# Copying transposed attention probabilities out of PSUM on two engines by turns

## The chip, the cores and the metric

The kernel runs on one core of a Trainium2 chip. That core has five engines that run beside each other, each with its own queue of instructions: TensorE (matrix products and transposes; in the profile PE, with PEld for its weight loads), VectorE (DVE), ScalarE (ACT), GpSimd (POOL) and SyncE (SP), which here issues DMAs. Matrix products land in PSUM, from where VectorE or ScalarE copies them to SBUF. The metric is the device time of one execution in microseconds (us); the figure for a kernel is the median of several executions.

## What is computed

Two layers of gated cross attention and feed forward on `x` of shape (2, 2048, 512) with a context of 128 rows per batch. The part that matters here is the first cross attention, with 16 heads of width 32 and biases on queries, keys and values:

```
q = (LN(x) Wq + bq) in 16 heads          # 2 x 2048 rows
k, v = ctx Wkv + bkv in 16 heads         # 2 x 128 rows
att = softmax(q k^T / sqrt(32)) over the 128 context rows
x = x + tanh(g_xattn[0]) * ((att v) Wo + bo)
```

After it `x` goes to a layer that picks 256 rows of each batch by a router score, runs self attention and a feed forward on them, and adds the result back; then comes a second cross attention (16 heads of width 64, no bias), and a feed forward of 2048 hidden units with rounded weights and values.

## The kernel before

The rows of x are worked in 8 blocks of 512 rows (4 tiles of 128). `cross_attention` (L215 on) is one function for both attentions; the flag `bias` is true for the first and false for the second. It loops over U, which counts heads over all blocks: 16 heads per block, 128 in all. One turn of the loop does these steps, for heads at different points of their way:

- `scores` (L268): TensorE multiplies queries by keys into `sc`. In the first attention four heads share a 128-row slice of the queries, so that the scores of four heads are made at once.
- `probabilities` (L285) calls `softmax_rows` (L116): VectorE takes the negated row maxima `nmx` (L119); ScalarE does four exponentials with running sums `den` (L122); VectorE inverts them into `rden` (L130); GpSimd multiplies `A` by `rden` (L131).
- Once per block `front` (L234) normalizes and transposes the rows of the next block; once per group of four heads `queries` (L246) makes `qT`, which ScalarE scales out of PSUM (L261).
- `transposed` (L291), two heads behind: TensorE transposes the four 128 x 128 pieces of `A` into one PSUM tile `tp` (L294), and `tp` is copied to `AT` in SBUF (L295).
- `values` (L297), after each fourth head: TensorE multiplies the four `AT` by the values into `po` (L302), and ScalarE copies `po` to `OT` (L310).
- `back` (L312), at the end of a block, in pieces: the output product `pp` (L320) and the gated residual sum (L329).
- `beside`: other work that is slipped in between. In the first attention this is the router (`router`, L795): statistics (L804, L805), scores (L808), the rows stored and the next rows loaded (L785, L832, L839), then the ranking of rows by comparisons on VectorE (`marks` L860, `tie` L904), and for the first batch's picked rows the self attention (L445 on).

The PSUM tiles `tp` and `po` come from one pool `ps_o` with two buffers (tag "o"; L741), and the router's `pb`, `old`, `new`, `pi` use the same two. `AT` has six SBUF buffers. A buffer is written again only when its last reader is done, so a transpose waits for the copy of the tile two before it.

The kernel is written against a tile framework that sets all waits between engines, and its planner fixes the order of every engine's queue ahead of the run. That order differs from the order of the program text: the trace shows, for example, the maxima of two later heads in VectorE's queue before the reciprocal of an earlier one. Each queue then runs in the order given.

Of the kernel before, what the change touches and what calls it, by code (L numbers as in the profile page):

```python
# [43 lines left out]
def flamingo_kernel(ctx: ExitStack, tc: tile.TileContext, a: dict, out: bass.AP):  # L44
    nc = tc.nc
# [169 lines left out]
    def cross_attention(  # L215
# [8 lines left out]
        L, nE, bias = W.L, W.nE, W.bias  # L224
# [9 lines left out]
        def front(n):  # L234

            tiles, xn, residual = rows_of(n)
            mv, rstd = ln_stats(tiles, L + "ln")
            for i, t in enumerate(tiles):
                normalize(xn[i], t, mv, rstd, i)
            xnT = act.tile([P, DC, BLK], F32, name="xnT", tag="xnT", bufs=xnT_bufs)  # L240
            transpose_block(
                ps_mm, "mm", xn, lambda d, pt: nc.scalar.copy(xnT[:, d, :], pt)
            )
            return residual, xnT

        def queries(xnT, grp):  # L246

            qT = [act.tile([P, BLK], F32, name="qT", tag="qT", bufs=3) for _ in range(cpg)]
            for c in range(cpg):
                e = grp * cpg + c  # L250
                pq = ps_mm.tile([P, BLK], F32, name="pq", tag="mm")
                for d in range(DC):
                    nc.tensor.matmul(  # L253
                        pq,
                        W.wq[:, d, ts(e, P)],
                        xnT[:, d, :],
                        start=(d == 0),
                        stop=(d == DC - 1),
                    )
                if bias:  # L260
                    nc.scalar.activation(  # L261
                        qT[c], pq, AF.Identity, scale=scale, bias=W.bq[:, e : e + 1]
                    )
                else:
                    nc.scalar.activation(qT[c], pq, AF.Copy, scale=scale)
            return qT

        def scores(b, qT, e):  # L268

            sc = [ps_sc.tile([P, TB, M], F32, name="sc", tag="sc") for _ in range(hpc)]
            for t in range(TB):
                for h in range(hpc):
                    r = slice(h * dh, (h + 1) * dh)
                    nc.tensor.matmul(  # L276
                        sc[h][:, t, :],
                        qT[e % cpg][r, ts(t, P)],
                        W.kT[r, b, e, :],
                        start=True,  # L280
                        stop=True,
                    )
            return sc

        def probabilities(sc):  # L285

            A = act.tile([P, TB, M], F32, name="A", tag="A", bufs=4)
            softmax_rows(sc, TB, M, act, row, A)
            return A

        def transposed(A, AT):  # L291
            tp = ps_o.tile([P, TB, P], F32, name="tp", tag="o")
            for t in range(TB):
                nc.tensor.transpose(tp[:, t, :], A[:, t, :], ident)  # L294
            nc.vector.tensor_copy(AT, tp.rearrange("p t n -> p (t n)"))  # L295

        def values(b, AT, OT, grp):  # L297
            for c in range(cpg):
                po = ps_o.tile([P, BLK], F32, name="po", tag="o")
                for h in range(hpc):  # L300
                    hd = grp * 4 + c * hpc + h
                    nc.tensor.matmul(  # L302
                        po[h * dh : (h + 1) * dh, :],
                        W.v[:, b, ts(hd, dh)],
                        AT[c * hpc + h],
                        start=True,
                        stop=True,
                    )
                OT.append(hold.tile([P, BLK], F32, name="OT", tag="OT", bufs=nE + cpg))
                nc.scalar.copy(OT[-1], po)  # L310

        def back(n, residual, OT):  # L312

            tiles = residual()
            for t in tiles:
                tc.keep_in_program_order(nc.gpsimd.tensor_tensor(t, t, W.bo, ALU.add))
            for i, t in enumerate(tiles):
                pp = ps_mm.tile([P, D], F32, name="pp", tag="mm")
                for e in range(nE):
                    nc.tensor.matmul(  # L320
                        pp,
                        OT[e][:, ts(i, P)],
                        W.wo[:, e, :],
                        start=(e == 0),
                        stop=(e == nE - 1),
                    )
                    if e == nE // 2 - 1:
                        yield
                nc.vector.scalar_tensor_tensor(t, pp, W.g, t, ALU.mult, ALU.add)  # L329
                if i == TB - 1:  # L330
                    after_block(n, tiles)
                yield
# [9 lines left out]
        As, AT, OT, out_of = {}, {}, {}, iter(())  # L342
        for U in range(N * H + 12):
            n, u = divmod(U, H)
            if n < N:
                grp, t = divmod(u, 4)
                if t == 0:
                    qT = next_qT
                if u % hpc == 0:
                    sc = scores(n // NBLK, qT, u // hpc)  # L350
                As[U] = probabilities(sc[u % hpc])
                if u == ahead and n + 1 < N:
                    residual[n + 1], xnT[n + 1] = front(n + 1)
                if t == 1 and grp < 3:
                    next_qT = queries(xnT[n], grp + 1)
                elif t == 1 and n + 1 < N:
                    next_qT = queries(xnT[n + 1], 0)
            V = U - 2
            if 0 <= V < N * H:
                AT[V] = act.tile([P, BLK], F32, name="AT", tag="AT", bufs=6)  # L360
                transposed(As.pop(V), AT[V])
            V = U - 4
            if 0 <= V < N * H and V % 4 == 3:
                n, grp = divmod(V // 4, 4)
                if grp == 0:
                    OT[n] = []
                values(n // NBLK, [AT.pop(i) for i in range(V - 3, V + 1)], OT[n], grp)
                if grp == 3:
                    out_of = back(n, residual.pop(n), OT.pop(n))
                    if n == N - 1:  # L370
                        after_units()
            next(out_of, None)
            beside(u)
# [369 lines left out]
    with ExitStack() as st:  # L743
# [43 lines left out]
        def beside(u):  # L787

            for _ in range(2):
                while pending and next(pending[0], pending) is pending:  # L790
                    pending.pop(0)
            for q in selecting:
                next(q, None)
# [211 lines left out]
        def stage1_rows(n):  # L1005
            tiles = [x[t] for t in range(n * TB, (n + 1) * TB)]
            xn = [act.tile([P, D], F32, name="xn", tag="xn", bufs=TB) for _ in tiles]
            return tiles, xn, lambda: tiles

        cross_attention(  # L1010
            W0, act, act, ps_mm, ps_sc, ps_o, row, 1, 10, stage1_rows,
            lambda n, tiles: pending.append(router(n, tiles)), beside,
# [319 lines left out]
    def quantize_hidden(g):  # L1332
# [27 lines left out]
        for c in range(HC):  # L1360
# [10 lines left out]
            if c % 2:  # L1371
                yield

    cross_attention(
        W1, act, hold, ps_mm, psum_pool(units, "L1_sc", 3), psum_pool(units, "L1_o", 2), row,
        1, 10, stage3_rows, stage3_done, beside4, second_half_starts,
# [51 lines left out]
    for g in range(LAST + 1):  # L1428
# [5 lines left out]
        for i in range(TB):  # L1434
            t, r, p = ahead.pop(0)
# [78 lines left out]
```

## Time and profile before

| | us |
|---|---|
| median of 3 executions | 1804.85 (1802.63 to 1807.84) |
| profiled execution, its own time | 1800.29 |
| its span, first to last instruction | 1798.6 |
| busy in the span: PE / DVE / ACT / POOL | 1648.9 / 1282.8 / 1070.5 / 537.6 |
| granted TensorE clock, mean | 0.967 of full |
| first copy `AT` starts; last copy of the first attention starts | 42.1; 542.4 |
| last copy `AT` of the second attention starts | 1574.7 |

Busy time is the sum of the durations of an engine's instructions; the ends of matrix products are modelled. Idle time of an engine counts only where something on the way to the end waits for it. The profile also gives, for each group of instructions of one line, the mean duration and what ended the idle time before them ("releaser"), and a chain of waits: starting at the last instruction, at each step back to what released it, or to the instruction before it on its engine. In the timelines "x4" stands for four like instructions in a row, taken together.

### The profile page before, as it was taken

To read this page: it belongs to the slowest core of one execution; us is meant where nothing else is said; L and a number is where in the kernel's file an instruction comes from. 1 tells how busy PE (TensorE), PEld (TensorE's weight loads), DVE (VectorE), ACT (ScalarE), POOL (GpSimd) and SP (SyncE) were. 2 spreads that over 40 slices of the span, in tenths; PEclk is the share of its full clock that TensorE was granted. 3 is DMA by queue.
4 is the path that set the end of the run, shared out by engine and by line. 5 is a ranking of instruction groups with operands and counts; after the bars stand their busy time and mean duration, and the time that the engine had idled before them with its cause. 6 is when DMAs were issued, how large, how long until landed. Compare 5 with 4: busy or idle time off the path is not lost.

```text
span 1798.6 us, 25225 instructions
## 1 busy us (share of the span) xinstructions
PE 1648.9 (92%) x8076; PEld 866.4 (48%) x8122; DVE 1282.8 (71%) x2608; ACT 1070.5 (60%) x3106; POOL 537.6 (30%) x671
## 2 busy tenths in 40 slices
PE   6998888989999988999999999999999999888969
PEld 3544444445455655755454544445444454434423
DVE  4676888966767534345358888798798879786967
ACT  2755456445453323435367878788788788744566
POOL 2534443432431012023224242342424324231200
PEclk9999999989889989999999999999999999998989
DMA  6011111121015880730011334234243133256375
GB/s 214 7 65 48 42 60 65 36 88 53 19 42 162 292 268 1 247 86 24 18 54 70 115 100 144 88 126 144 79 150 100 77 115 109 88 187 238 133 237 188
DMA packets 119828, 196.99 MB, mean 110 GB/s; under 512 B 12900, under 2 KB 50532, under 8 KB 115984
## 3 DMA queue, kind: packets, MB, share of 16 engines
q1 hardware_dynamic: 117872, 192.23, 31.2%
q0 software_dynamic: 960, 2.10, 0.6%
q8 instruction: 64, 1.05, 0.2%
q10 hardware_dynamic: 864, 1.05, 0.2%
q14 instruction: 68, 0.56, 0.1%
HBM read 120.89 MB, written 74.45 MB: 109 GB/s over the span
## 4 chain that ended last, share of the span: by engine, by line
PE 56%; DVE 23%; DMA 8%; ACT 6%; POOL 3%; issue 2%; SPq 0%; ACTq 0%; DVEq 0%; POOLq 0%
PE pp L320 14%; PE pq L253 12%; PE po L302 4%; PE sc L276 4%; PE tp L294 4%; PE ph L1157 3%; DVE h L1173 3%; DVE AT L295 2%; ACT A L122 2%; DVE nmx L119 2%; PE po L1386 2%; DVE marks L860 2%; PE pu L646 2%; PE acc L631 2%; PE pw L646 2%
## 5 line engine op out<-in xcount | busy, mean ns | idle before, releaser
L122 ACT ACTIVATE A<-sc,nmx 128x128 f32<-128x128 f32 x1024 | 363.2, 382 | 143.1 <-DVE nmx L119 129.5
L131 POOL TENSOR_TENSOR A<-A,rden 128x512 f32<-128x512 f32 x256 | 277.2, 1085 | 512.4 <-DVE rden L130 402.4
L320 PE MATMUL pp<-L_wo,OT 128*128 128x512 f32 x768 | 367.5, 610 | 16.6 <-DVE x L329 11.2
L253 PE MATMUL pq<-xnT,L_wq 128*128 128x512 f32 x768 | 346.6, 599 | 11.4 <-DVE x L329 11.4
L122 ACT ACTIVATION_READ_ACCUMULATOR A<-sc,nmx 128x1 f32 x1024 | 227.1, 222 | 0.0
L253 PEld LDWEIGHTS pq<-xnT,L_wq 128*128 128x128 f32 x768 | 143.2, 192 | 171.7 <-issue 151.0
L119 DVE TENSOR_REDUCE nmx<-sc 128x4 f32<-128x512 f32 x256 | 168.9, 679 | 69.8 <-PE sc L276 69.8
L320 PEld LDWEIGHTS pp<-L_wo,OT 128*128 128x128 f32 x768 | 136.7, 193 | 162.6 <-issue 132.8
L295 DVE COPY AT<-tp 128x512 f32<-128x512 f32 x256 | 172.9, 680 | 57.8 <-PE tp L294 56.9
L1173 DVE SCALAR_TENSOR_TENSOR h<-u,cw,h 128x512 f32<-128x512 f32 x256 | 204.5, 834 | 5.9 <-ACT h L1169 5.5
L294 PE MATMUL tp<-ident,A 128*128 128x128 f32 x1024 | 164.5, 284 | 25.4 <-POOL A L131 13.9
L294 PEld LDWEIGHTS tp<-ident,A 128*128 128x128 f32 x1024 | 118.2, 143 | 96.4 <-issue 46.0
L276 PEld LDWEIGHTS sc<-L_kT,qT 32*128 32x128 f32 (+1 forms) x2048 | 110.8, 190 | 75.8 <-issue 56.6
L276 PE MATMUL sc<-L_kT,qT 32*128 32x128 f32 (+1 forms) x2048 | 138.2, 292 | 6.5 <-ACT A L122 4.6
L1386 PE MATMUL po<-w2q,hq 128*128 128x512 bf16 x501 | 120.8, 393 | 18.4 <-DVE hq L1368 8.3
L1169 ACT ACTIVATE h<-u,cb,cw 128x512 f32<-128x512 f32 x128 | 99.1, 808 | 64.7 <-DVE u L1167 56.6
L1157 PE MATMUL ph<-xiT,w1q 128*128 128x512 bf16 x477 | 122.3, 379 | 3.8 <-DVE u L1167 1.8
L302 PE MATMUL po<-AT,L_v 128*32 128x512 f32 (+1 forms) x512 | 117.6, 646 | 7.7 <-DVE AT L295 6.2
L1167 DVE TENSOR_TENSOR u<-ph,inv_b 128x512 f32<-128x512 f32 x128 | 85.1, 684 | 31.5 <-PE ph L1157 27.5
L1166 POOL COPY u<-carry 128x2 f32<-128x2 f32 x128 | 49.7, 390 | 166.9 <-DVE h L1173 140.9
L310 ACT COPY OT<-po 128x512 f32<-128x512 f32 x96 | 56.0, 590 | 64.9 <-PE po L302 64.6
L1168 POOL COPY carry<-u 128x2 f32<-128x2 f32 x128 | 48.7, 385 | 149.7 <-DVE u L1167 147.9
(237 smaller groups left out, 2310.2 us busy)
## 6 DMA issues: line engine op xcount, KB each, us to landing
h_d<-h SPq DMA_DIRECT2D x28, 1024.0 KB, 4.4
x_d<-x SPq DMA_DIRECT2D x64, 256.0 KB, 3.2
hf<-h_d SPq DMA_DIRECT2D x64, 256.0 KB, 3.4
x<-x_d SPq DMA_DIRECT2D x61, 256.0 KB, 4.4
x<-h_d SPq DMA_DIRECT2D x48, 256.0 KB, 5.2
x_d<-xo SPq DMA_DIRECT2D x32, 256.0 KB, 2.0
xf<-x_d SPq DMA_DIRECT2D x32, 256.0 KB, 3.5
hq_d<-hi SPq DMA_DIRECT2D x64, 128.0 KB, 1.8
```

The lines of the kernel that those rows point to most:

```text
L119: nc.vector.tensor_reduce(nmx, sc, AX.X, ALU.max, negate=True)
L122: nc.scalar.activation(out_tile[:, h, :], sc[:, h, :], AF.Exp, bias=nmx[:, h : h + 1], accum_out=den[:, h : h + 1],)
L131: nc.gpsimd.tensor_tensor(out_tile, out_tile, rden.unsqueeze(2).to_broadcast([P, n, width]), ALU.mult,)
L253: nc.tensor.matmul(pq, W.wq[:, d, ts(e, P)], xnT[:, d, :], start=(d == 0), stop=(d == DC - 1),)
L276: nc.tensor.matmul(sc[h][:, t, :], qT[e % cpg][r, ts(t, P)], W.kT[r, b, e, :], start=True, stop=True,)
L294: nc.tensor.transpose(tp[:, t, :], A[:, t, :], ident)
L295: nc.vector.tensor_copy(AT, tp.rearrange("p t n -> p (t n)"))
L302: nc.tensor.matmul(po[h * dh : (h + 1) * dh, :], W.v[:, b, ts(hd, dh)], AT[c * hpc + h], start=True, stop=True,)
L320: nc.tensor.matmul(pp, OT[e][:, ts(i, P)], W.wo[:, e, :], start=(e == 0), stop=(e == nE - 1),)
L1157: nc.tensor.matmul(ph, w1q[:, d, ts(c, P)], xiT[g][:, d, :], start=(d == 0), stop=(d == DC - 1),)
L1173: nc.vector.scalar_tensor_tensor(z, u[:, ds(k, BLK)], cw[:, c, k : k + 1], z, ALU.mult, ALU.add)
L1386: nc.tensor.matmul(po, rows(c), w2q[:, c, :], start=(c == 0), stop=(c == HC - 1))
```

## The change

`transposed` gets the copying instruction as an argument. In the first attention (`bias` true) heads with an odd number V are copied by ScalarE's copy; heads with an even number, and all heads of the second attention, are copied by VectorE as they were.

```diff
-        def transposed(A, AT):
+        def transposed(A, AT, copy):
             tp = ps_o.tile([P, TB, P], F32, name="tp", tag="o")
             for t in range(TB):
                 nc.tensor.transpose(tp[:, t, :], A[:, t, :], ident)
-            nc.vector.tensor_copy(AT, tp.rearrange("p t n -> p (t n)"))
+            copy(AT, tp.rearrange("p t n -> p (t n)"))
...
             V = U - 2
             if 0 <= V < N * H:
                 AT[V] = act.tile([P, BLK], F32, name="AT", tag="AT", bufs=6)
-                transposed(As.pop(V), AT[V])
+
+                copy = nc.scalar.copy if bias and V % 2 else nc.vector.tensor_copy
+                transposed(As.pop(V), AT[V], copy)
```

No other line differs. The copies have the same shape, 128 x 512 in float32, and the same source and target tiles.

## The prediction

> **What bounds the kernel now.** I read the busy table of the page first: over the whole span TensorE is busy 92%, VectorE 71%, ScalarE 60%. The change touches only the first cross attention, so these means say little, and I cut the span by time. The 128 heads of that stage put their copies `AT` between 42 and 542 us. Busy time in three stretches, in the order PE, PEld, DVE, ACT, POOL, then granted clock, DMA share and GB/s:
>
> ```profile
> 45.00:180.00 135.00, 122.37 (x809) 65.53 (x808) 94.22 (x217) 87.29 (x394) 59.25 (x56) 0.99 0.11 40
> 180.00:360.00 180.00, 157.33 (x1026) 82.23 (x1022) 154.27 (x335) 94.38 (x415) 76.61 (x66) 0.98 0.15 51
> 360.00:540.00 180.00, 162.73 (x910) 90.17 (x911) 118.65 (x279) 91.21 (x383) 65.84 (x62) 0.90 0.15 51
> ```
>
> TensorE works 442.4 of these 495 us, so 52.6 us are the most that any relief of other engines could bring here. From 180 to 360 us VectorE is as full as TensorE (154.3 beside 157.3 of 180) and ScalarE is half empty (94.4). The two engines that the change trades between are thus unequal, and most so there.
>
> Then the groups of the page, for prices (operation, shapes, count | busy us, mean ns | idle before):
>
> ```profile
> L122 ACT ACTIVATE A<-sc,nmx 128x128 f32<-128x128 f32 x1024 | 363.2, 382 | 143.1 <-DVE nmx L119 129.5
> ...
> L295 DVE COPY AT<-tp 128x512 f32<-128x512 f32 x256 | 172.9, 680 | 57.8 <-PE tp L294 56.9
> ...
> L310 ACT COPY OT<-po 128x512 f32<-128x512 f32 x96 | 56.0, 590 | 64.9 <-PE po L302 64.6
> ```
>
> L295 is the copy that moves; L310 is the same shape, PSUM to SBUF, already done by ScalarE.
>
> Third, the chain of waits from 40 to 530 us, listed whole: PE holds 239 of its 491 us, DVE 140, ACT 45. L295 is on it with 35 copies, 21.4 us. I numbered the copies in order of time (the k-th is head k): 23 are odd heads, 12 even. The pieces look like this (start, us, what):
>
> ```profile
> 226.70 0.69 DVE ln_st L804
> 227.40 0.59 DVE AT L295
> 227.98 0.09 DVE ln_mv L805
> 228.07 0.58 DVE ws L808 x2
> ...
> 237.11 0.06 DVE rden L130
> 237.18 0.59 DVE AT L295
> 237.76 0.14 issue
> 237.90 0.63 PE tp L294 x4
> ...
> 265.84 0.60 DVE AT L295
> 266.44 0.60 DVE L_ln_st L99
> ```
>
> The first and the last (heads 57, 67) stand between VectorE's own instructions: nobody waits for that `AT`, it only holds up what is queued behind it. The middle one (head 59) is a real dependency: its buffer of the two-buffer PSUM pool is what the next transposes need. Of the 23 odd copies 16 are of the first kind, 7 of the second (heads 11, 27, 43, 47, 59, 75, 97).
>
> Fourth, who keeps TensorE waiting from 45 to 540 us (total us, times, longest):
>
> ```profile
> PE pp L320 <- DVE x L329: 10.8, 3, 4.3
> PE tp L294 <- POOL A L131: 10.4, 8, 3.2
> PE tp L294 <- DVE AT L295: 9.0, 8, 2.0
> ```
>
> So VectorE's queue, and not the length of one copy, is what TensorE feels: a residual add that comes late, a normalization whose `rden` came late, a copy that came late.
>
> **The change, part by part.** *Removed from VectorE*: 64 copies (odd V, first attention only). One lasts 0.68 us by its row, but the next instruction begins 0.60 us after it in the chain, so its place in the queue costs 0.60: 64 x 0.60 = 38.4 us, a tenth of the 367.15 us that the table gives VectorE.
>
> *Added to ScalarE*: 64 copies at 0.59 us (L310). What one occupies is read where it stands among exponentials:
>
> ```profile
> 242.72 0.21 ACT L122 ACTIVATION_READ_ACCUMULATOR A<-sc,nmx 128x1 f32 x1
> 242.81 0.60 ACT L873 COPY sb<-pb 128x512 f32<-128x512 f32 x1
> 243.28 0.40 ACT L122 ACTIVATE A<-sc,nmx 128x128 f32<-128x128 f32 x1
> ```
>
> The next one starts 0.47 us later: 64 x 0.47 = 30 us, so ScalarE goes from 272.88 to about 303 of 495 us, 61%. It does not become the bound. That L873 copy lies between two exponentials with nothing loaded in between, so the alternation itself is free.
>
> A rule speaks against this trade. The Trainium skill, "ScalarE: Activation LUTs", section "Rules for kernel authors", gives plain arithmetic to VectorE because VectorE is faster per element. By the rule each moved copy would be slower than the one it replaces. The rows say the opposite for this source: 590 ns on ScalarE beside 680 ns on VectorE, 0.09 us less. I take the rows. By the rule the 7 dependent copies would lose something each; by the rows they gain 7 x 0.09 = 0.6 us before queues are counted.
>
> *The 16 queue pieces on the chain.* Each leaves VectorE's queue and nothing has to follow at once: 16 x 0.60 = 9.6 us. What is late next? In the stretch about head 57 the chain runs on from L808 through POOL's `ln_rstd`, ScalarE's `xo`, a store and a load of x, to L99; VectorE waits 1.3 us for that load, TensorE 0.98 us for POOL and 1.46 us for `AT` there. A gain of 0.6 us fits under these waits. In the stretch from 252 to 272 us VectorE is full, TensorE idles 2.88 and 1.22 us; again 0.6 to 1.2 us fit. So little is cut off, and I take 8 of the 9.6 us.
>
> *The 7 dependent pieces.* The timeline has the transposes of head 59 end at 233.93 us, but the copy starts at 237.09: 3.2 us in VectorE's queue, behind maxima and L99. ScalarE ends the exponentials of head 61 at 234.75 (head 61 is what stands before this copy in program order), so there it would run from about 234.8 to 235.3. The next transposes then wait for POOL's `A` of head 61 (done at 237.53) instead and start 0.37 us earlier than their 237.90. Heads 27, 43 and 75 are the same place in other blocks: 4 x 0.37 = 1.5 us. Head 97 waits 4.5 us for VectorE and holds TensorE's L81 for 2.3 us of its own waits; head 47 holds L866 for 1.2 us, and head 11's copy begins 0.8 us after its transposes end. Best case: 1.5 + 2.3 + 1.2 + 0.8 = 5.8 us gained. Worst case: the planner puts these copies behind the exponentials of heads 62 and 63 (end 238.1), so that they end 0.75 us later than now: 7 x 0.75 = 5 us lost. I take -2, nearer to the first end, since the copy stands before those exponentials in program order.
>
> *The wait that is added to ScalarE.* A copy waits for PE's transposes, and behind it on ScalarE stand the exponentials of the next heads, a `qT` eviction or an `xo`; for these wait VectorE's `rden`, POOL's `A` and in the end transposes three heads on. The Trainium skill, "PSUM — Partial Sum Buffer", section "Engine vs sequencer instructions", calls ScalarE's queue strictly first in, first out, so nothing passes a waiting copy; that rule speaks against the change. To price it I went through all odd heads V in the timeline, with the copy put behind the exponentials of V+2, and asked how late those of V+3 become. In 29 places they are held, by 0.4 to 5 us and once 11.9 us, 65 us in all. By the rule alone, with every hold on the path, that is the loss. By the rows it is slack: between the end of POOL's `A` of head V+3 and the start of its transposes lie 1.2 us and more at every one of these places, and in 28 of the 29 that is more than the hold (head 19: 3.1 us held, 6.8 us of slack; head 59: 0.8 and 2.0). ScalarE runs ahead of TensorE, so a hold costs nothing until it exceeds that lead. The one place over (head 87) is at zero. I take 0, with 10 us as the far end.
>
> *The order.* The instructions are not in program order in the trace (the maxima of two later heads stand before the reciprocal of an earlier one): a planner lays out every queue, and other engines in these copies make it lay out anew. No view shows the new order. I bound it at -4 to +8 us and take +1.
>
> Sum: -8 - 2 + 0 + 1 = **-9 us**. The profiled execution took 1800.29 us (span 1798.6 and 1.7 around it), so it would take 1791.3. The median of the runs shown, 1804.85, lies 4.6 us above the profiled one; the same 9 us from it give **1795.8 us**. The rest of the kernel is not edited, and starts when this stage lets it.
>
> **The rivals.**
>
> *Covered (same).* TensorE, 89% busy here, swallows it: the queue pieces go, but the transposes then wait for POOL's `A` (10.4 us already). For it: POOL's A is the releaser in the table above, and head 59 shows it 0.37 us behind. Against it: POOL waits for `rden`, which is VectorE's too. A third of the gain: 1802.
>
> *ScalarE's queue (slower).* The holds fall on the path, because the lead that covers them is itself used up: VectorE's `rden` comes a hold later, POOL's `A` after it, and each hold eats the lead of the next group. It decides where more than 9 us of the 65 us of holds come through; with a third, 21 us, it is net +12: 1817. For it: at heads 4k the transposes already follow POOL's `A` within 0.1 us in several blocks (heads 28, 44, 60, 76), so there is no lead left at those; the transposes' buffers turn over in two. Against it: at just these places ScalarE sits idle before the exponentials (it waits 85 us of 490 for VectorE's `nmx`), so the copy goes into a gap.
>
> *More than the chain shows (faster).* All of VectorE's waits shrink with its load: a tenth off its 367 us takes a third of the 31 us or so that VectorE's instructions keep TensorE waiting, with the late residual adds, and the dependent copies their 5.8: 15 to 20 us, 1787.
>
> *It does not do what it says:* the flag `bias` is set for the first attention alone, and V odd is half the heads; I see no way around that.
>
> **How the numbers follow.** About 0.3% (5.4 us) is what a measurement of this kernel can tell from no change. My forecast has 0.40, its own range 1791 to 1800; a gain below 5.4 us belongs to "same". Covered 0.20, ScalarE's queue or a worse order 0.25, more than the chain 0.15. Of the forecast's 0.40 some 0.03 fall short of 5.4 us: faster 0.52, same 0.23, slower 0.25. The range for 8 in 10 reaches to 1783 on the side of the bigger gain and to 1818 on the side of ScalarE's queue, whose case then lies about half inside.
>
> **What would show it.** VectorE's busy time from 45 to 540 us lower by about 43 us, ScalarE's higher by about 38 (durations overlap, so more than the 38.4 and 30 of the queues); L295 split into 192 DVE and 64 ACT copies of 0.59 us. Right: the stage's last copy earlier by about 9 us, pairs like L804, L295, L805 without the middle one, fewer waits of PE for DVE. Wrong: a row of ACT waiting for `PE tp L294` of tens of us, `DVE rden` waiting longer for `ACT A`, PE waiting longer for `POOL A`; or a stage of the same length with a new releaser.

## The result, and the profile after

The changed kernel takes 1791.58 us (median of 8 executions, 1789.39 to 1796.68) beside 1803.14 us for the kernel before (8 executions, 1798.66 to 1811.35): ratio 0.9935 with a 95% interval from 0.9915 to 0.9954, that is 11.7 us (0.65%) less. The prediction said 9 us less. The profiled execution took 1791.24 us with a span of 1789.2.

The exponentials' group of the page after the change (count | busy us, mean ns | idle before and its releaser):

```profile
L122 ACT ACTIVATE A<-sc,nmx 128x128 f32<-128x128 f32 x1024 | 363.8, 385 | 131.5 <-DVE nmx L119 121.7
```

Line 295 by itself after the change (count: shortest/median/longest ns, first and last start):

```profile
L295 DVE COPY AT<-tp x192: 650/680/693, 42.8 to 1561.3; 128x512 f32<-128x512 f32 x192
L295 ACT COPY AT<-tp x64: 577/596/697, 45.1 to 529.4; 128x512 f32<-128x512 f32 x64
```

The count is as the diff says: 64 copies went, and each is shorter on the engine that took it. The exponentials of L122 cost what they cost before (385 ns beside 382), and ScalarE is idle 12 us less in front of them.

To see where the time came from, the same *work* has to be compared, not the same microseconds. The first stage ends where TensorE begins the first expert's product `pu`: at 565.97 us before, at 552.74 us after. The window of each kernel that ends there (start:end, length, then busy us of PE, PEld, DVE, ACT, POOL, granted clock, DMA share, GB/s), before:

```profile
0.00:566.00 566.00, 496.67 (x2985) 266.23 (x2986) 410.59 (x930) 288.31 (x1241) 216.72 (x215) 0.95 0.18 61
```

and after:

```profile
0.00:552.70 552.70, 491.53 (x2984) 264.27 (x2985) 376.12 (x866) 318.83 (x1305) 216.07 (x215) 0.95 0.18 62
```

VectorE's busy time fell by 34.5 us (0.54 for each copy), ScalarE's rose by 30.5 (0.48 each): columns of busy time count overlapping instructions once. TensorE did the same work, and the time in which it did nothing fell from 566.0 - 496.7 = 69.3 us to 61.2: 8.1 us. This **idle time of TensorE over equal work** is the measure that all experiments below are read by. The other 5 us of the 13.3 are TensorE's own busy time (496.7 to 491.5); that number lies between 493.8 and 502.9 us in the runs below that keep the TensorE queue of the kernel before, and of the 13.3 us only 9.4 are left at the end of the two spans (1798.6 to 1789.2).

Who keeps TensorE waiting after the change, 45 to 530 us (total us, times, longest):

```profile
PE pp L320 <- DVE x L329: 11.5, 4, 6.0
PE tp L294 <- POOL A L131: 10.6, 11, 2.1
PE po L302 <- DVE AT L295: 5.3, 5, 3.1
...
PE tp L294 <- ACT AT L295: 1.4, 2, 1.0
```

The row "tp from `AT`" was 9.0 us before; 1.4 are left of it, now for ScalarE. In sum the wait for POOL's `A` did not grow (10.4 before, 10.6 after), though at single places it did take the place of the wait for `AT`, as B_even's block below shows; and a part came back one product later, at `po` (5.3). The same view for ScalarE:

```profile
ACT AT L295 <- PE tp L294: 17.9, 16, 4.4
```

and for VectorE:

```profile
DVE rden L130 <- ACT A L122: 50.5, 32, 4.4
```

The first row is new, and the second was 23.0 us in 26 waits. So ScalarE is held by copies that wait for transposes, and VectorE then waits longer for exponentials. The prediction listed both rows as signs that it is wrong; the time fell all the same.

### The profile page after: what moved, and what is told of

Same layout as the page of the kernel before. It is cut to its first block, busy times and chain, and to the rows that moved or that the text cites. A ratio compares the mean times of both kernels' runs of the same rounds, so it can differ in the third digit from the quotient of the medians.

```text
span 1789.2 us, 25277 instructions
## 1 busy us (share of the span) xinstructions
PE 1647.3 (92%) x8122; PEld 864.8 (48%) x8122; DVE 1250.1 (70%) x2544; ACT 1101.7 (62%) x3170; POOL 536.0 (30%) x671
## 4 chain that ended last, share of the span: by engine, by line
PE 29%; DVE 15%; DMA 5%; ACT 4%; issue 2%; POOL 1%; SPq 1%; DVEq 0%; POOLq 0%; ACTq 0%
PE pq L253 8%; PE pp L320 8%; DVE h L1175 4%; PE po L302 3%; PE ph L1159 3%; PE sc L276 3%; PE po L1388 2%; PE tp L294 2%; DMA x<-h_d 1%; DVE u L1169 1%; DVE AT L295 1%; DVE nmx L119 1%; DMA hq<-hq_d 1%; DVE hf L1258 1%; DMA h_d<-h 1%
## 5 line engine op out<-in xcount | busy, mean ns | idle before, releaser
L122 ACT ACTIVATE A<-sc,nmx 128x128 f32<-128x128 f32 x1024 | 363.8, 385 | 131.5 <-DVE nmx L119 121.7
L131 POOL TENSOR_TENSOR A<-A,rden 128x512 f32<-128x512 f32 x256 | 275.9, 1079 | 506.7 <-DVE rden L130 410.8
L122 ACT ACTIVATION_READ_ACCUMULATOR A<-sc,nmx 128x1 f32 x1024 | 229.7, 224 | 0.0
L294 PE MATMUL tp<-ident,A 128*128 128x128 f32 x1024 | 164.4, 284 | 18.7 <-POOL A L131 13.2
L295 DVE COPY AT<-tp 128x512 f32<-128x512 f32 x192 | 129.8, 678 | 43.5 <-PE tp L294 42.8
L302 PE MATMUL po<-AT,L_v 128*32 128x512 f32 (+1 forms) x512 | 119.3, 657 | 11.7 <-DVE AT L295 11.1
L130 DVE RECIPROCAL rden<-den 128x4 f32<-128x4 f32 x256 | 43.3, 169 | 80.0 <-ACT A L122 72.8
```

Source lines behind the costliest of these rows:

```text
L122: nc.scalar.activation(out_tile[:, h, :], sc[:, h, :], AF.Exp, bias=nmx[:, h : h + 1], accum_out=den[:, h : h + 1],)
L131: nc.gpsimd.tensor_tensor(out_tile, out_tile, rden.unsqueeze(2).to_broadcast([P, n, width]), ALU.mult,)
L302: nc.tensor.matmul(po[h * dh : (h + 1) * dh, :], W.v[:, b, ts(hd, dh)], AT[c * hpc + h], start=True, stop=True,)
```

## The experiments

The theory on trial, **Q**: the gain is the place of 64 copies in VectorE's queue. Rivals: **D**, the odd heads' copies come earlier and free their PSUM buffer earlier, whatever VectorE's load; **O**, the planner's new order did it; **S**, the holds on ScalarE eat a part of what VectorE's relief brings. Every ratio is to the kernel before, run beside it on the same chip.

### First four: each laid out anew by the planner

*dveload*: the change, and VectorE gets other work back.

```diff
+                if bias and V % 2:
+                    scr = act.tile([P, BLK], F32, name="scr", tag="scr", bufs=1)
+                    A = A.rearrange("p t m -> p (t m)")
+                    nc.vector.tensor_tensor(scr, A, A, ALU.mult)
```

> The changed kernel, and for each odd head of the first attention VectorE also multiplies A by itself into a scratch tile (128 x 512, as long as a copy); the output is not touched. Theory Q (VectorE's queue: the gain is that 38 us of its queue are gone): the load is back, so the gain goes: 1800 to 1806 us beside 1803 before, ratio 0.998 to 1.003. Rival D (the odd copies themselves come earlier and free the two PSUM buffers sooner; VectorE's load does not matter): AT still comes from ScalarE, so the gain stays: 1791 to 1795, ratio 0.993 to 0.996. Rival P (the planner's new order was lucky): a third order, anything from 1785 to 1815.

*actload*: the kernel before, and ScalarE copies each odd head's finished `AT` once more, into a scratch tile.

```diff
+                if bias and V % 2:
+                    scr = act.tile([P, BLK], F32, name="scr", tag="scr", bufs=1)
+                    nc.scalar.copy(scr, AT[V])
```

> The kernel before, and for each odd head of the first attention ScalarE also copies AT into a scratch tile, so it gets the 64 waits and the 30 us of the change while VectorE keeps its 64 copies; the output is not touched. Theory Q, by which ScalarE's holds lie in slack: no change, 1801 to 1806 us, ratio 0.999 to 1.002. Rival S (the holds on ScalarE cost, and the change gained net of them): slower, 1809 to 1820, ratio 1.003 to 1.010.

*free*: the odd heads' copies are left out altogether; their products use the even neighbour's `AT`.

```diff
+                if bias and V % 2:
+                    AT[V] = AT[V - 1]
+                transposed(As.pop(V), AT[V], (lambda to, tp: None) if bias and V % 2 else nc.vector.tensor_copy)
```

> The changed kernel without the 64 odd copies: an odd head of the first attention is multiplied with the AT of the even head before it, so its output is not the reference's. Neither engine pays for them. Theory Q: about what the change gives, since ScalarE's part was in slack and only the 7 dependent copies get shorter: 1785 to 1791 us, ratio 0.990 to 0.994. Rival S (ScalarE's copies and holds cost a part of the gain): well below, 1770 to 1783, ratio 0.982 to 0.989.

*even*: the even heads' copies on ScalarE.

```diff
-                copy = nc.scalar.copy if bias and V % 2 else nc.vector.tensor_copy
+                copy = nc.scalar.copy if bias and V % 2 == 0 else nc.vector.tensor_copy
```

> The even heads of the first attention go to ScalarE, the odd ones stay on VectorE. The relief of VectorE is the same 38 us. By the chain of waits of before (23 odd copies on it, 12 even) Theory Q gives about half: 1795 to 1799 us, ratio 0.995 to 0.998. Rival D: the even copies are the buffers of other transposes and hardly waited for: 1800 to 1804. Rival L (only the sum of VectorE's load counts, not which copies): as the change, 1790 to 1793, ratio 0.993 to 0.994.

| | ratio to before, 95% interval |
|---|---|
| dveload | 1.0043 [1.0026, 1.0060] |
| actload | 1.0048 [1.0030, 1.0065] |
| free | 1.0021 [1.0010, 1.0031] |
| even | 1.0044 [1.0026, 1.0061] |

All four are slower than the kernel before, `free` too, in which neither engine makes the copies. By Q alone that can't be. The queues of actload differ from those before in few places; its 8.7 us are then probably for the most part what 64 more copies cost ScalarE where VectorE is not relieved (they also keep the `AT` buffers longer), but with an order that is not quite the same that isn't shown. In the other three, stretches of TensorE's and VectorE's queues stand otherwise than before, all within the first stage. They don't tell Q from O.

### Four with the order held

So the planner's order was written down and held. The five queues of one kernel are recorded as lists of instruction numbers, and each instruction is tied to the one ahead of it by an edge that sets no semaphore:

```diff
+    for queue in queues_of(ORDER):
+        for a, b in zip(queue, queue[1:]):
+            tc.add_manual_dep(
+                traced[b],
+                traced[a].name,
+                mybir.DependencyInfo(mybir.DependencyClass.NoSync, mybir.DependencyReason.DATA),
+                reason="order",
+            )
```

Names beginning with B hold the order of the kernel before, with A that of the kernel after; a moved copy stands in its new queue where the plan has it in time. *B_act*: order of before, odd copies on ScalarE. *A_dve*: order of after, odd copies back on VectorE. *B_free*, *A_free*: the odd copies left out as in `free`, in either order.

> The kernel before with its order of instructions written down and held on all five engines; only the 64 odd copies are taken out of VectorE's queue and put into ScalarE's, each behind the same ScalarE instruction as in the changed kernel. So the planner has no part in it. Theory Q (relief of VectorE's queue): 1790 to 1797 us, ratio 0.993 to 0.997. Rival P (the change gained by the planner's new order, of which even, dveload and free drew worse ones): 1801 to 1808, ratio 0.999 to 1.003.

> The changed kernel's order held on all five engines, with the 64 odd copies back in VectorE's queue, at the place in time where the plan has them on ScalarE. Theory Q: the relief is gone, 1801 to 1810 us, ratio 0.999 to 1.004. Rival P: the order alone carries the gain, 1790 to 1796, ratio 0.993 to 0.996.

> The changed kernel's order held on all five engines, with the 64 odd copies left out; an odd head takes the AT of the even head before it, so its output is not the reference's. Theory Q with ScalarE in slack: hardly below the changed kernel, 1786 to 1792 us, ratio 0.990 to 0.994. Rival S (ScalarE's copies and the waits in its queue cost a part of the gain): 1775 to 1784, ratio 0.984 to 0.989.

> The order of the kernel before held on all five engines, with the 64 odd copies left out, heads as in A_free; its output is not the reference's. This is the most that the relief can bring without a new order. Theory Q: 1786 to 1794 us, ratio 0.990 to 0.995; and B_act lies within 4 us of it. Rival P: 1799 to 1805, ratio 0.997 to 1.001.

| | ratio, 95% interval | first stage, us | TensorE busy in it | idle |
|---|---|---|---|---|
| before | 1 | 566.0 | 496.7 | 69.3 |
| after | 0.9935 [0.9915, 0.9954] | 552.7 | 491.5 | 61.2 |
| B_act | 0.9932 [0.9916, 0.9949] | 559.6 | 498.2 | 61.4 |
| A_dve | 0.9995 [0.9978, 1.0013] | 564.9 | 493.4 | 71.5 |
| B_free | 0.9928 [0.9911, 0.9945] | 556.5 | 496.2 | 60.3 |
| A_free | 0.9902 [0.9886, 0.9918] | 549.8 | 489.5 | 60.3 |

The idle column comes out of lines like this one, the window of B_act up to its first `pu` product (559.60 - 498.23 = 61.4):

```profile
0.00:559.60 559.60, 498.23 (x2984) 267.50 (x2985) 376.11 (x866) 319.71 (x1305) 216.82 (x215) 0.95 0.18 61
```

This settles O: the edit with the old order brings the whole gain (0.9932), the new order without the edit brings nothing (0.9995). It bounds S as well. Leaving the copies out takes them from VectorE and gives ScalarE nothing, and that is 0.0004 better than B_act in the one order and 0.0033 better than after in the other: 0.7 and 6 us, each with about 4.5 us of uncertainty, and 1 us of TensorE's idle time. With VectorE relieved, ScalarE's part costs between nothing and some 6 us. The busy column shows why it isn't read as a gain: before and B_act do the same TensorE work in the same queue and differ by 1.5 us there, after and B_act by 6.7, with equal ratios. One rival remains for B_act's number: its six executions were granted a clock of 0.969 in the median, the kernel before beside it 0.964, so a part of its 12.3 us can be the clock. Its idle time is 8 us shorter all the same, and the gain is there without a higher clock in B_free (0.9655) and in the changed kernel (0.965).

TensorE's waits show the same thing. B_act, 45 to 530 us:

```profile
PE tp L294 <- POOL A L131: 11.5, 11, 2.8
```

and A_dve:

```profile
PE tp L294 <- DVE AT L295: 13.2, 9, 2.3
```

With the copies on VectorE, TensorE's transposes wait for an `AT` in either order, 9.0 and 13.2 us; with them on ScalarE that row is gone but for 0.5 us in B_act and 1.4 in after.

### Four more in a held order: which heads, how many, what load

*B_even*: as B_act, but with the even heads. *B_q1*: only the 32 heads 4k+1. *A_all*: order of after, all 128 heads of the first attention. *B_dvl*: B_act with a multiply that nobody reads at each old place on VectorE.

```diff
 B_even
-                copy = nc.scalar.copy if bias and V % 2 else nc.vector.tensor_copy
+                copy = nc.scalar.copy if bias and V % 2 == 0 else nc.vector.tensor_copy
 B_q1
+                copy = nc.scalar.copy if bias and V % 4 == 1 else nc.vector.tensor_copy
 A_all
+                copy = nc.scalar.copy if bias else nc.vector.tensor_copy
 B_dvl
+                if bias and V % 2:
+                    scr = act.tile([P, BLK], F32, name="scr", tag="scr", bufs=1)
+                    nc.vector.tensor_tensor(scr, W.bo, W.bo, ALU.mult)
```

> Order of the kernel before, written down and held on all five engines; the 64 copies of the even heads are ScalarE's, those of the odd heads stay VectorE's. Theory Q as the chain of waits read it (the gain is what the pieces of the moved copies hold in the chain: 12 even pieces of 0.6 us, about 7 us, less than the 23 pieces of the odd heads): ratio about 0.996. Theory L (the gain is VectorE's load as a whole, 64 copies of 0.60 us less, whichever heads they belong to; the chain's pieces are not a list of what can be gained): like the odd heads under this order, 0.9932, so 0.992 to 0.9945. Near 1.000 would say that the place of the odd heads is what matters.

> Order of the kernel before, held; only the 32 heads 4k+1 have their copy on ScalarE. By the pieces of the chain of waits (11 of the 16 queue pieces and one dependent piece are theirs): 7 to 8 us, ratio about 0.9957. By load alone (half the copies): half of 0.68%, 0.9965 (0.9955 to 0.9975). If the dependent pieces matter most (six of seven are heads 4k+3): 0.998 to 1.000.

> Order of the kernel after, written down and held; all 128 copies of the first cross attention are ScalarE's (64 more than in the change), VectorE's queue is 64 copies shorter still. If VectorE still holds TensorE at the even heads' copies (waits of 5.3 us for them are left in the profile of after, and the load of 64 copies was worth 0.68%): 0.988 to 0.9925, better than both kernels. If nothing more is to be had there: 0.993 to 0.995. Rival (ScalarE's slack is used up: about 333 of 490 us busy, every softmax exponential stands behind a copy that waits for TensorE): 0.996 to 1.004.

> As B_act (order of the kernel before, held; the odd heads' copies on ScalarE), with one more VectorE multiply per odd head (W.bo times itself, SBUF to SBUF, 128x512, read by nobody) at the place in VectorE's queue which that head's copy had. So the copies stay moved, and VectorE's queue is as long as before. Theory Q/L (the gain is the queue place on VectorE): it is given back, ratio 0.998 to 1.001 (the multiply waits for nothing, so it may take a little less place than the copy that waited for TensorE). Rival (the gain is that an odd head's transposes no longer wait for a copy that stands in VectorE's order, whatever VectorE's length): it is kept, 0.992 to 0.995.

| | ratio, 95% interval | idle of TensorE in the first stage |
|---|---|---|
| B_even | 1.0042 [1.0026, 1.0057] | 571.0 - 496.8 = 74.2 |
| B_q1 | 0.9950 [0.9931, 0.9970] | 558.2 - 493.8 = 64.4 |
| A_all | 0.9947 [0.9917, 0.9978] | 556.4 - 492.8 = 63.6 |
| B_dvl | 1.0027 [1.0013, 1.0042] | 574.6 - 502.9 = 71.7 |

**B_even** is the miss that teaches most: the same load moved, the same order held, 7.6 us lost where 12.3 were won, and neither reading of Q allows for it. It can be seen where a block begins. TensorE's first waits of the block at 176 us, before (start, us, what, [idle before it, and the releaser]):

```profile
175.89 0.66 PE L294 MATMUL tp<-ident,A 128*128 128x128 f32 x4 [0.98 <-POOL A L131]
178.59 0.63 PE L294 MATMUL tp<-ident,A 128*128 128x128 f32 x4 [1.18 <-DVE AT L295]
```

in B_act:

```profile
174.75 0.66 PE L294 MATMUL tp<-ident,A 128*128 128x128 f32 x4 [0.52 <-POOL A L131]
177.26 0.65 PE L294 MATMUL tp<-ident,A 128*128 128x128 f32 x4 [1.00 <-POOL A L131]
```

and in B_even:

```profile
179.79 0.66 PE L294 MATMUL tp<-ident,A 128*128 128x128 f32 x4 [1.47 <-POOL A L131]
182.19 0.63 PE L294 MATMUL tp<-ident,A 128*128 128x128 f32 x4 [0.89 <-DVE AT L295]
```

The first wait (transposes of head 44) is for the way from scores to `A`, and here ScalarE has no lead: 0.98 us before, 0.52 with the odd copies moved, 1.47 with the even ones. It repeats at the blocks that begin at 117, 176, 235 and 295 us (0.98 or 0.99 before; 0.52 or 0.53; 1.47 each), and at 525 us it is 3.22, 2.77 and 3.72. The half microsecond is one copy. B_even's timeline of ScalarE, VectorE and GpSimd there:

```profile
176.35 0.35 ACT L122 ACTIVATE A<-sc,nmx 128x128 f32<-128x128 f32 x1
...
176.69 0.35 ACT L122 ACTIVATE A<-sc,nmx 128x128 f32<-128x128 f32 x1
...
177.03 0.57 ACT L295 COPY AT<-tp 128x512 f32<-128x512 f32 x1
177.50 0.38 ACT L122 ACTIVATE A<-sc,nmx 128x128 f32<-128x128 f32 x1
...
178.34 0.18 DVE L130 RECIPROCAL rden<-den 128x4 f32<-128x4 f32 x1 [1.67 <-ACT A L122]
...
178.69 1.04 POOL L131 TENSOR_TENSOR A<-A,rden 128x512 f32<-128x512 f32 x1 [4.48 <-DVE rden L130]
```

The copy of head 42 stands between the second and the third exponential of head 44, the very head that TensorE waits for: 177.03 to 177.50, 0.47 us, go straight through `rden` and `A` to the transposes at 179.79. In B_act the four exponentials of that head follow each other at 171.79, 172.13, 172.47 and 172.82 with no copy between them. So B_even adds a hold where there is no slack. Five such places make some 2.5 us of the 4.9 us by which its idle time exceeds that of before; the rest is the balance of waits that are longer or shorter elsewhere, by up to 1.3 us each, which I could not pin to one cause.

The second wait is for the copy of head 43, on VectorE, before (1.18 us) and in B_even (0.89). In B_act that copy is ScalarE's, and TensorE waits for POOL's `A` instead, 1.00 us: the copy comes earlier, and what was next in line holds the transposes almost as long. Over the four blocks from 117 to 295 us these second waits sum to 4.9 us before, 5.2 in B_act, 4.3 after and 3.7 in B_even, so the row of waits for `AT` that vanished is not gain as a whole.

That a copy stands in the middle of a head is B_even's held plan; `even`, planned freely, has other places and is as slow (1.0044), and why that one is was not taken apart.

**B_q1** has half of the copies and 9.0 us (5.4 to 12.5) beside B_act's 12.3. The 7 to 8 us that the chain's pieces gave lie in this interval, and the load-only value of 0.9965 too, so the two readings are not told apart; the reading that all lies in the heads 4k+3 is excluded. Its row of transposes that wait for `AT` is as long as before (8.9 us, 9.0 before), and it gains all the same; its row for POOL's `A` is 7.9 us instead of 10.4.

**A_all** is no better than after. VectorE's load falls by another 36 us in the window (376.12 to 340.53), and TensorE's row for POOL's `A` rises from 10.6 to 15.1 us, with 1.03 us at the block's first transposes instead of 0.54: the even copies cost there what they cost in B_even. No version tried beats the change; A_free does, but it leaves out half of the copies; B_act equals the change. A_all doesn't say that VectorE's further relief is worth nothing: the relief and the price of the even copies come together in it.

**B_dvl** gives all of the gain back and 5 us more, although the copies stay on ScalarE. That speaks against D, but the total does not decide it, for the multiply was a heavier load than the copy. Its row in B_dvl:

```profile
L366 DVE TENSOR_TENSOR scr<-L_bo x64: 652/680/1766, 43.4 to 550.7; 128x512 f32<-128x512 f32 x64
```

and GpSimd's normalization beside it (groups, 40 to 560 us), in B_dvl

```profile
L131 POOL TENSOR_TENSOR A<-A,rden 128x512 f32<-128x512 f32 x128 | 147.6, 1157 | 239.1 <-DVE rden L130 207.4 <-DVE m L540 11.2 <-PE tp L294 9.1
```

and before:

```profile
L131 POOL TENSOR_TENSOR A<-A,rden 128x512 f32<-128x512 f32 x128 | 137.7, 1079 | 235.8 <-DVE rden L130 188.7 <-DVE m L535 11.9 <-PE tp L294 9.7
```

A multiply takes up to 1.77 us (the mean of the 64 is 800 ns), and the normalizations grow by 9.9 us in sum, on the way to `tp`. So a part of what was given back, and the 5 us beyond the kernel before, can be this, or the holds on ScalarE without VectorE's relief; the shares stay open. In `dveload` the multiply is of the same kind (its mean 823 ns), which is one reason why that run was slower than the kernel before.

The beginning of a block is free of this, and there Q can be told from D. Before, the copy of head 41 stands in VectorE's queue between L804 and L805; from L805 the way leads over the router's few short steps, ScalarE's `xo`, the exponentials of head 44, `rden` and `A` to the first wait above. VectorE before:

```profile
167.68 0.69 DVE L804 BATCH_NORM_STATS2 ln_st<-x 128x6 f32<-128x512 f32 x1
168.28 0.67 DVE L295 COPY AT<-tp 128x512 f32<-128x512 f32 x1
168.88 0.17 DVE L805 BATCH_NORM_AGGREGATE ln_mv<-ln_st 128x2 f32<-128x6 f32 x1
```

in B_act (two lines lower in its file):

```profile
166.99 0.69 DVE L806 BATCH_NORM_STATS2 ln_st<-x 128x6 f32<-128x512 f32 x1
167.72 0.18 DVE L807 BATCH_NORM_AGGREGATE ln_mv<-ln_st 128x2 f32<-128x6 f32 x1
```

and in B_dvl, with TensorE's first wait of the block:

```profile
171.17 0.69 DVE L809 BATCH_NORM_STATS2 ln_st<-x 128x6 f32<-128x512 f32 x1
171.78 0.68 DVE L366 TENSOR_TENSOR scr<-L_bo 128x512 f32<-128x512 f32 x1
172.38 0.17 DVE L810 BATCH_NORM_AGGREGATE ln_mv<-ln_st 128x2 f32<-128x6 f32 x1
...
179.39 0.66 PE L294 MATMUL tp<-ident,A 128*128 128x128 f32 x4 [0.98 <-POOL A L131]
```

From one statistic to the next VectorE takes 1.20 us before, 0.73 without the copy and 1.21 with the multiply in its place, and TensorE's wait goes with it: 0.98, 0.52 and 0.98. The multiply is not a long one here (0.68 us), the normalization that TensorE waits for lasts 1.04 us in all three, and in B_dvl the copies are ScalarE's as in B_act. So at this place it is VectorE's queue and not a buffer that comes free earlier. At the other four places (117, 235, 295 and 525 us) B_dvl has 1.00, 0.98, 0.99 and 3.23 us, the waits of the kernel before again. The five make 2.3 us of the 8 us by which B_act's idle time is shorter; for the rest Q and D are not told apart.

Open too is `free`. With its own order it lies 0.9% over B_free and 1.2% over A_free, which make the same instructions: some 17 and 21 us for an order alone. Its stage has *less* idle time than that of before (568.7 - 503.7 = 65.0 us), yet TensorE is busy 7 us longer for the same products, at a granted clock of 0.93 instead of 0.95. That is not the chance of one profile: over the whole kernel the 22 executions of `free` were granted 0.959 in the median (0.955 to 0.964), the 32 of the kernel before beside it 0.9645 (0.960 to 0.969), and the same instructions in the two held orders 0.9655 (B_free) and 0.966 (A_free). So the lower clock comes with this kernel in this order; what in the order brings it, and how much of the 17 us it makes, stays open.

## Why the prediction was right, step by step

*The bound.* TensorE, with VectorE's queue as what it feels: right. Its idle time over equal work fell 8.1 us and the row of waits for `AT` from 9.0 to 1.4, though not all of that row is gain (5.3 us came back at `po`, and POOL's `A` takes over in most of the second waits). The stage's last copy comes 13.0 us earlier (542.4 to 529.4) where about 9 were promised; TensorE's shorter busy time is in that.

*VectorE's relief and ScalarE's load.* Places of 0.60 and 0.47 us: measured 0.54 and 0.48 by the busy columns of equal work. But the signs of 43 and 38 us that the last paragraph promised were sums of durations, and the columns don't count an overlap twice: 34.5 and 30.5. The section's own queue places were the better estimate.

*Queue pieces and dependent pieces.* -8 and -2, -10 together; alone, in the old order, they measure -12.3 us (B_act, interval -9.2 to -15.2). The mechanism of the queue pieces is seen where the prediction put it: heads 25, 41, 57, 73 and 121, five of the 16, are the copies between L804 and L805, and each shortens TensorE's wait by 0.45 to 0.46 us where 0.60 was put. The other eleven were not read one by one; B_q1, which has 11 of the 16 and one dependent piece, brings 9.0 (5.4 to 12.5). Of the dependent pieces, heads 27, 43, 59 and 75 were to give 1.5 us, as POOL's `A` comes next 0.37 us earlier; the second waits behind them sum to 4.9 us before and 4.3 after, a gain of 0.6, and to 5.2 in B_act, no gain. The waits at L81 (2.3 us, head 97) and L866 (1.2 us, head 47) are gone in B_act but for 0.5 and 0.3 us, and a product near L81 (`pq`) waits 1.8 us longer there. So -2 was too much for the first four, and that the sum came out so near is in part luck.

*The rule weighed.* The rows were right to be preferred: the copy lasts 596 ns on ScalarE beside 680 ns on VectorE after the change. But the rule was read too widely. The row of the Trainium skill, "ScalarE: Activation LUTs", section "Rules for kernel authors", names `relu`, `max`, `min`, `add` and `mul` and says of bf16 that VectorE is faster per element; it gives nothing for float32 copies out of PSUM, so these rows don't contradict it.

*The holds on ScalarE.* Taken at 0 with 10 us as the far end; 0.7 and 6 us by the two pairs with the copies left out, so the term was right in size or short by a few microseconds; `actload`, 8.7 us slower, hints at a higher price where VectorE is not relieved. The reason given holds for the odd heads: ScalarE's lead covers them. That the holds would show as longer waits of VectorE for `A` was listed as a sign of failure, and it was a poor sign: 50.5 us of such waits cost nothing while TensorE's row for POOL's `A` stays at 10.6. The rival that named heads 4k, where no lead is left, named the right place: the first waits above are those of heads 28, 44, 60 and 76. But no odd copy came to stand among the exponentials of head 44 in B_act; in B_even the copy of head 42 does, and that is the price, 0.49 us each time.

*The order.* Taken at +1 in a range of -4 to +8: A_dve measures -0.9 us (-4.0 to +2.3). Right here, but the range was too narrow for what an order can do: the same instructions as B_free took 17 us more in the order of `free`.

*The rivals.* Covered: true at most of the second waits, where POOL's `A` takes over, and in part at `po` (5.3 us), but not of the whole. More than the chain: the 15 to 20 us were not reached (11.7, interval 8.3 to 15.3), yet A_free, where ScalarE does not pay for the copies, gains 17.7 (14.8 to 20.6), so the reading is not excluded; A_all can't decide it.

## What to carry to other kernels

Before an instruction moves to a less busy engine, look at the instructions it will stand in front of there and at how far that engine is ahead of the bound at that point: 64 copies of the odd heads won 12 us, and the 64 of the even heads, the same load, lost 8 at the places they were given. The chain of waits says what holds the end now on the engine that gives, and nothing of the engine that takes. And where a planner lays out the queues, hold the order before reading an experiment, and compare the bound engine's idle time over equal work; otherwise an effect of 1% from the order hides the one that is looked for.

## What the hardware showed unasked

A 128x512 multiply from SBUF to SBUF on VectorE and GpSimd's instructions of the same size lengthen each other (the multiply up to 1766 ns for a median of 680, GpSimd's normalization 1157 instead of 1079 ns in the mean), while the copy out of PSUM that it replaced never took over 693 ns. In B_dvl each of the 17 multiplies that lasted over 0.8 us overlaps a GpSimd instruction in time; the other 47 lasted at most 0.70 us. The Trainium skill, "GPSIMD Engine Reference", section "1. Specifications", lists the SBUF interface as shared with VectorE, with contention where a VectorE instruction has two SBUF inputs; the multiply has two and the copy none, and the rows agree. A probe that replaces a copy by a multiply is therefore not the same load.
